# The output loop of a linear attention, reordered from two stages to three

## The chip, the cores and the metric

The kernel runs on one core of a Trainium2 chip. The core has five engines with a queue of instructions each, which they work off in order: TensorE (PE, matrix products and transposes into the PSUM memory), VectorE (DVE), ScalarE (ACT), GpSimd (POOL) and SyncE (SP, which here issues transfers). They wait for one another through semaphores. The metric is the time of one execution on the device in microseconds (us), the median of the runs.

## The reference

The input x has 4 images of 256 channels and 64 x 64 pixels, in fp32. Four layers follow, each of the form x = x + layer(groupnorm(x)):

- layer 0: a 3x3 convolution with group norm and ReLU, and on it an attention of every pixel to every pixel (4096 x 4096 logits per image, 128 channels) whose output goes through a 1x1 convolution and a group norm
- layer 1: a linear attention with 4 heads of 32 channels; this is the layer that the change touches
- layer 2: a depthwise 3x3 and a pointwise convolution with weights generated from the input
- layer 3: a pointwise convolution with a mix of 4 experts' weights

The core of layer 1:

```
xn = rmsnorm(x, g_norm)
q, k, v = split(einsum('oc,bchw->bohw', w_qkv, xn))
q = softmax(q, axis=-2); k = softmax(k, axis=-1)
context = einsum('bhdn,bhen->bhde', k, v)
out = einsum('bhde,bhdn->bhen', context, q * scale)
out = einsum('oc,bchw->bohw', w_out, out) + b_out
return rmsnorm(out, g_out)
```

The last line divides each pixel's 256 outputs by their norm. The kernel folds context and w_out into one matrix w2, so that the output of a pixel is q times w2, then takes its norm, scales by the inverse, and adds the result to x. That last part is the output loop.

## The kernel before

**Two streams of work.** The attention of layer 0 is the largest part. `attend(b)` (L596 to L659) is a generator: each step is one iteration, made of two logits matmuls (`pf`, L606), two exponentials on ACT (L607), two matmuls with the values (`py`, L645) and one running sum on DVE (`tot`). Everything else of an image, the convolution ahead of the attention and the three layers behind it (`tail`), is a second stream, written as generators that say `yield n` between their pieces. `Chain` (L39 to L78) turns each `yield n` into a credit of n times a rate, and for every whole credit one attention iteration is put between the pieces. There is no planner behind it: the order in which the program writes the instructions is the order in each engine's queue (`manual_schedule`, L1099).

**The runs.** While attention of image 0 runs, image 1 is convolved (rate 1.5). With attention of image 1 come the layers 1 to 3 of image 0 and the convolution of image 2 (rate 0.86), and with attention of image 2 the layers of image 1 and the convolution of image 3 (0.86). With attention of image 3 come the layers of image 2 (rate 1.24). The layers of image 3 come last and have no attention beside them; `alone` is true there.

**The output loop** (L791 to L836) goes over 8 chunks of 512 pixels. It has three functions:

- `outputs(c)`: four products of q with w2 go to two PSUM banks (`ps_o`, L799), ACT squares them and accumulates each pixel's sum of squares into `zr` (L801, four squares), DVE takes the maximum with 1e-24 (L803), and POOL raises it to the power -1/2 (`rsqrt`, L187; the page shows it as L189)
- `scaled(zr, banks)`: `z` is the product times `zr`, read from the two `ps_o` banks, as two operations on DVE (L814, shown as L109); with `alone` the first half is done by ACT instead (L812)
- `added(c, z)`: for each half of the channels four transposes of `z` into a bank (`ps_zt`, L822), then on DVE the sum with the residual (L823, shown as L112) and its statistics (`bn_stats`, L824)

One turn writes outputs(c), a `yield 0.6`, added(c-1), scaled(c) and another `yield 0.6`. After the last turn come a `yield 1` and added(7). After the loop the statistics of the layer are aggregated (`mv`, L276) and averaged over the group by two small matmuls on PE (`pm`, L281, and `pv`, L290), with which layer 2 begins.

**Buffers.** All banks of PSUM come from one pool of 8 (L106): `pf`, `py`, `ps_o`, `ps_zt` and the rest. The first writer of a bank waits until the last reader of its previous content is done. `zr` has three buffers, `z` comes from a pool of ten (`k4`, L95) or, alone, from alternating spare memory, and `junk` (the squares that nobody reads) has one.

Of the kernel before, what the change touches and what calls it, by code (L numbers as in the profile page):

```python
# [81 lines left out]
def conv_preact_fast(ctx: ExitStack, tc: tile.TileContext, guard, x, wc, wtpg, ww, wqkv, wout, w1cat, wd2,  # L82
# [11 lines left out]
    def k4(name):  # L94
        return wk.tile([P, CH], F32, tag="k4", name=name, bufs=10)  # L95
# [6 lines left out]
    def junk():  # L102
        return wk.tile([P, 512], F32, tag="junk", name="junk")

    def bank(name):
        return pp.tile([P, 512], F32, tag="bank", name=name, bufs=8)  # L106

    def tt(o, a, b, op):
        nc.vector.tensor_tensor(o, a, b, op)  # L109

    def stt(o, a, s, b, op0, op1):
        nc.vector.scalar_tensor_tensor(o, a, s, b, op0, op1)  # L112
# [74 lines left out]
    def rsqrt(o, v):  # L187

        nc.gpsimd.tensor_tensor(o, v, half[:, 0:v.shape[1]], ALU.pow)  # L189
# [510 lines left out]
    def linear_attention(w, b, big, qT, k4, st, sh, alone):  # L700
# [4 lines left out]
        NC = N // 512  # L705
# [54 lines left out]
        last = None  # L760
        for c in range(NC):
# [8 lines left out]
            last = this  # L770
# [22 lines left out]
        def outputs(c):  # L793
            zr = sp.tile([P, 4], F32, name="zr", bufs=3)
            banks = []
            for s in range(2):
                ps = bank("ps_o").rearrange("p (j o) -> p j o", j=2)
                for j in range(2):
                    nc.tensor.matmul(ps[:, j, :], qT[:, bass.ts(4 * c + 2 * s + j, P)], w2, start=True, stop=True)  # L799
                for j in range(2):  # L800
                    nc.scalar.activation(junk()[:, 0:NH * P], ps[:, j, :], AF.Square, accum_out=zr[:, 2 * s + j:2 * s + j + 1])  # L801
                banks.append(ps)
            nc.vector.tensor_scalar(zr, zr, 1e-24, None, ALU.max)  # L803
            rsqrt(zr, zr)
            return zr, banks

        def scaled(zr, banks):
            z = k4("z").rearrange("p (j o) -> p j o", j=4)
            for s in range(2):
                if alone and s == 0:  # L810
                    for j in range(2):
                        nc.scalar.activation(z[:, j, :], banks[0][:, j, :], AF.Copy, scale=zr[:, j:j + 1])  # L812
                    continue
                tt(z[:, bass.ts(s, 2), :], banks[s], zr[:, bass.ts(s, 2)].unsqueeze(2).to_broadcast([P, 2, NH * P]), ALU.mult)  # L814
            return z

        def added(c, z):
            cols = bass.ts(c, 512)
            for h in range(NH):
                pt = bank("ps_zt")  # L820
                for j in range(4):
                    nc.tensor.transpose(pt[:, bass.ts(j, P)], z[:, j, bass.ts(h, P)], ident)  # L822
                stt(big[:, h, cols], pt, gains[:, 1, h:h + 1], big[:, h, cols], ALU.mult, ALU.add)  # L823
                nc.vector.bn_stats(st[:, h, c, :], big[:, h, cols])  # L824

        last = None
        for c in range(NC):
            zb = outputs(c)
            yield 0.6
            if last is not None:  # L830
                added(c - 1, last)
            last = scaled(*zb)
            yield 0.6
        yield 1
        added(NC - 1, last)
        return st  # L836


# [222 lines left out]
    def tail(b, big, qT, k4=k4, diag=None, xs_in=None, held=None):  # L1061

        def layers(w):
            st, sh = yield from nonlocal_out(w, b, big, k4, xs_in)
            st = yield from linear_attention(w, b, big, qT, k4, st, sh, diag is not None)
            st, sh = yield from generated(w, b, big, k4, st, sh, diag)
            if b + 2 < B:
                load_x(b + 2)
            elif b + 2 == B:
                for h in range(NH):  # L1070
                    for q in range(2):
                        half_image = bass.ts(q, N // 2)
                        nc.sync.dma_start(out=x_cols[:, h, half_image], in_=xs_d[b + 1, h, :, half_image])
            yield from mixed(w, b, big, k4, st, sh, held)
        return layers
# [23 lines left out]
    with tc.manual_schedule(engines={E.PE, E.Activation, E.DVE, E.Pool, E.SP}):  # L1099
# [19 lines left out]
        last = end.steps()  # L1119
# [596 lines left out]
```

## Time and profile before

| | before |
|---|---|
| median of 3 runs (lowest, highest) | 3239.0 us (3237.38, 3240.34) |
| profiled execution: own time, span | 3238.86 us, 3237.0 us |
| mean clock granted to TensorE | 0.982 |
| busy: PE, DVE, ACT, POOL | 95%, 64%, 35%, 4% |
| chain that ended last: PE, DVE | 78%, 14% |
| output loop of images 0 and 1, products of chunk 0 to the aggregation | 56.2, 56.7 us |
| output loop of image 2 | 62 us |
| output loop of image 3, without attention | 39.7 us |

The span is the time from the first to the last instruction of the profiled execution; 1.9 us of its own time lie around it. A busy share is an average over stages with different limits. The stretch of the output loop of images 0 to 2 holds attention iterations of the next image as well, so its length is no measure of the loop alone.

In a line of a timeline the columns are start, duration, engine, source line, operation, output<-input, shapes, a count, and in brackets how long the engine was idle before it and which instruction ended that. A helper's line stands for all its calls: L109 is every `tt`, L112 every `stt`. Matmuls are pipelined, so the duration of a group of them overlaps the next.

### The profile page before, as it was taken

Reading aid. Unit: us, or ns where it says so; the run is one execution under the profiler, and the core shown is the slowest. Engines: PE = TensorE matmul, PEld = TensorE weight load, DVE = VectorE, ACT = ScalarE, POOL = GpSimd, SP = SyncE. Lnnn points to the kernel's source line nnn. Section 1 sums busy time; section 2 is a strip of 40 time slices with the busy share of each in tenths; the row PEclk is TensorE's granted clock in tenths of the full one; section 3 lists DMA queues with packets and bytes.
Section 4 is the critical chain, followed back from the end, with each engine's and each line's share of the span. In section 5 each row is a group of like instructions: output and inputs, shape, how many; then the busy total and the mean of one; then the engine's idle time right before and its main releaser. Section 6 shows DMA issues by size and latency. Waiting matters only on the chain.

```text
span 3237.0 us, 24205 instructions
## 1 busy us (share of the span) xinstructions
PE 3082.0 (95%) x8494; PEld 1480.6 (46%) x8494; DVE 2075.6 (64%) x2603; ACT 1146.4 (35%) x2139; POOL 129.3 (4%) x169
## 2 busy tenths in 40 slices
PE   6899989999999999999999999999999999996797
PEld 3354434445554444444465344444555534443533
DVE  8646675342546995786537796778353768855575
ACT  2232224333555332223364532222355453333520
POOL 0000000000010000000011000000000100000100
PEclk9999999999999999999999999999999999997998
DMA  5510103001100013113300102211410010121101
GB/s 178 177 36 30 33 30 59 7 13 46 66 11 20 20 72 117 36 36 65 111 10 1 39 20 82 101 44 33 107 59 1 10 33 13 46 72 46 49 0 73
DMA packets 73792, 161.66 MB, mean 50 GB/s; under 512 B 7744, under 2 KB 39232, under 8 KB 70720
## 3 DMA queue, kind: packets, MB, share of 16 engines
q1 hardware_dynamic: 69056, 143.27, 12.9%
q0 software_dynamic: 4608, 16.78, 2.9%
q8 instruction: 69, 1.13, 0.1%
q14 instruction: 59, 0.48, 0.0%
HBM read 103.40 MB, written 73.40 MB: 55 GB/s over the span
## 4 chain that ended last, share of the span: by engine, by line
PE 78%; DVE 14%; issue 5%; ACT 2%; DMA 0%; POOL 0%; SPq 0%; POOLq 0%; ACTq 0%
PE pf L606 23%; PE py L645 22%; PE ps_conv L380 8%; PE ps_qkv L734 5%; DVE dw L112 4%; PE ps_tp L582 3%; PE ps_ex L1045 3%; PE ps_pw L908 2%; DVE tot L109 2%; PE ps_g L587 2%; PE ps_h L867 2%; PE ps_wy L629 1%; PE ps_o L799 1%; DVE big L109 1%; DVE ra L112 1%
## 5 line engine op out<-in xcount | busy, mean ns | idle before, releaser
L607 ACT ACTIVATE pr<-pf 128x512 f32<-128x512 f32 x1024 | 604.0, 596 | 1241.1 <-PE pf L606 1234.0
L606 PE MATMUL pf<-tpg 128*128 128x512 f32 x2048 | 969.0, 595 | 2.8 <-ACT pr L607 2.8
L645 PE MATMUL py<-pr,tpg 128*128 128x512 f32 x2048 | 962.2, 592 | 2.9 <-ACT pr L607 2.7
L109 DVE TENSOR_TENSOR tot<-tot,pr 128x1024 f32<-128x1024 f32 x448 | 546.4, 1220 | 280.1 <-ACT pr L607 278.7
L645 PEld LDWEIGHTS py<-pr,tpg 128*128 128x128 f32 x2048 | 388.7, 190 | 494.5 <-issue 478.3
L606 PEld LDWEIGHTS pf<-tpg 128*128 128x128 f32 x2048 | 381.6, 190 | 451.4 <-issue 420.0
L380 PE MATMUL ps_conv<-v,u 128*128 128x512 f32 x576 | 267.3, 611 | 29.0 <-DVE v L109 25.1
L112 DVE SCALAR_TENSOR_TENSOR dw<-xp,dk,dw 128x1008 f32<-128x1008 f32 x224 | 282.9, 1267 | 7.0 <-ACT dw L900 3.7
L380 PEld LDWEIGHTS ps_conv<-v,u 128*128 128x128 f32 x576 | 112.0, 196 | 175.1 <-issue 141.8
L734 PE MATMUL ps_qkv<-wqkv_s,xg 128*128 128x384 f32 x384 | 130.8, 490 | 0.0
L582 PE MATMUL ps_tp<-big,wtpg_s 128*128 128x512 f32 x256 | 117.1, 601 | 3.0 <-ACT big L470 3.0
L189 POOL TENSOR_TENSOR rstd<-rstd,half 128x2 f32<-128x2 f32 x24 | 16.8, 700 | 2508.0 <-DVE rstd L292 2314.3
L109 DVE TENSOR_TENSOR tpg<-ps_g,bg_s 128x512 f32<-128x512 f32 x32 | 22.1, 691 | 146.0 <-PE ps_g L587 146.0
L908 PE MATMUL ps_pw<-dw,pk 128*128 128x512 f32 x224 | 103.8, 597 | 10.9 <-DVE dw L112 10.9
L620 DVE RECIPROCAL inv<-pss 128x512 f32<-128x512 f32 x32 | 107.2, 3351 | 8.0 <-PE pss L618 8.0
L734 PEld LDWEIGHTS ps_qkv<-wqkv_s,xg 128*128 128x128 f32 x384 | 72.2, 191 | 52.6 <-issue 8.9
L742 DVE TENSOR_REDUCE qs<-qk 128x16 f32<-128x512 f32 x24 | 16.5, 686 | 123.4 <-ACT qk L736 123.4
L109 DVE TENSOR_TENSOR v<-ra 128x1024 f32<-128x1024 f32 x72 | 86.8, 1218 | 0.4
L583 ACT ACTIVATE tpg<-ps_tp,btp_s 128x512 f32<-128x512 f32 x64 | 43.9, 687 | 119.2 <-PE ps_tp L582 119.1
L908 PEld LDWEIGHTS ps_pw<-dw,pk 128*128 128x128 f32 x224 | 42.7, 191 | 65.4 <-issue 50.9
L582 PEld LDWEIGHTS ps_tp<-big,wtpg_s 128*128 128x128 f32 x256 | 47.6, 193 | 54.5 <-issue 50.0
L801 ACT ACTIVATE junk<-ps_o 128x256 f32<-128x256 f32 x128 | 49.2, 384 | 64.5 <-PE ps_o L799 57.5
(273 smaller groups left out, 2948.3 us busy)
## 6 DMA issues: line engine op xcount, KB each, us to landing
u<-filters SPq DMA_DIRECT2D x144, 128.0 KB, 2.3
xp<-in_x_dram SPq DMA_DIRECT2D x16, 1024.0 KB, 6.4
xs_d<-big POOLq DMA_DIRECT2D x32, 512.0 KB, 11.2
wy_d<-wt SPq DMA_DIRECT2D x32, 512.0 KB, 3.0
out_dram<-res SPq DMA_DIRECT2D x64, 256.0 KB, 2.0
wy<-wy_d SPq DMA_DIRECT2D x28, 512.0 KB, 5.2
xs<-xs_d SPq DMA_DIRECT2D x24, 512.0 KB, 5.3
wp<-in_wp_dram SPq DMA_DIRECT2D x16, 512.0 KB, 4.6
```

What stands on the lines that cost most here:

```text
L109: nc.vector.tensor_tensor(o, a, b, op)
L112: nc.vector.scalar_tensor_tensor(o, a, s, b, op0, op1)
L380: nc.tensor.matmul(ps[oh], u(oh, h), v[:, bass.ts(h, 512)], start=(h == 0), stop=(h == NH - 1))
L582: nc.tensor.matmul(ps, wtpg_s[:, h, k, :], big[:, h, cols], start=(h == 0), stop=(h == NH - 1))
L587: nc.tensor.matmul(ps[:, j, :], big[:, h, bass.ts(4 * c + j, P)], wtpg_s[:, h, 2, :], start=(h == 0), stop=(h == NH - 1))
L606: nc.tensor.matmul(pf, phi[:, bass.ts(2 * m + s, P)], theta[:, bass.ts(q, 512)], start=True, stop=True)
L607: nc.scalar.activation(pr[:, bass.ts(s, 512)], pf, AF.Exp)
L620: nc.vector.reciprocal(inv, pss)
L645: nc.tensor.matmul(py, g[:, bass.ts(2 * m + s, P)], probs[i][:, bass.ts(s, 512)], start=(m == 0 and s == 0), stop=(m == NM - 1 and s == 1))
L734: nc.tensor.matmul(ps[:, 0:3 * HID], xg[:, h, bass.ts(j, P)], wqkv_s[:, h, :], start=(h == 0), stop=(h == NH - 1))
L908: nc.tensor.matmul(ps, pk[:, h * NH * P + oh * P:h * NH * P + (oh + 1) * P], dw[h][:, bass.ts(s, 512)], start=(h == 0), stop=(h == NH - 1))
L1045: nc.tensor.matmul(ps, wm[h][:, bass.ts(oh, P)], big[:, h, cols], start=(h == 0), stop=(h == NH - 1))
```

## The change

`outputs(c)` ends with the squares. The maximum and the power become a function of their own, `inverse(zr)`. The loop runs two turns longer: a turn writes the products and squares of chunk c, then the sums of chunk c-2, then the inverse of chunk c and the scaling of chunk c-1. In the two added turns only the parts that are left are written, with one `yield 0.6` each; the `yield 1` ahead of the last sums is gone. The credits of the loop go from 8 x 1.2 + 1 = 10.6 to 8 x 1.2 + 2 x 0.6 = 10.8. The two `ps_o` banks of a chunk are read by its scaling one turn later. The instructions themselves are the same.

```diff
                     nc.scalar.activation(junk()[:, 0:NH * P], ps[:, j, :], AF.Square, accum_out=zr[:, 2 * s + j:2 * s + j + 1])
                 banks.append(ps)
+            return zr, banks
+
+        def inverse(zr):
             nc.vector.tensor_scalar(zr, zr, 1e-24, None, ALU.max)
             rsqrt(zr, zr)
-            return zr, banks
...
-        last = None
-        for c in range(NC):
-            zb = outputs(c)
+        zb, z = {}, {}
+        for c in range(NC + 2):
+            if c < NC:
+                zb[c] = outputs(c)
+                yield 0.6
+            if c > 1:
+                added(c - 2, z.pop(c - 2))
+            if c < NC:
+                inverse(zb[c][0])
+            if 0 < c <= NC:
+                z[c - 1] = scaled(*zb.pop(c - 1))
             yield 0.6
-            if last is not None:
-                added(c - 1, last)
-            last = scaled(*zb)
-            yield 0.6
-        yield 1
-        added(NC - 1, last)
         return st
```

## The prediction

> **What bounds the kernel now.** I read the shares of busy time first, then windows laid on the four executions of the output loop, then the timelines of TensorE (PE) and VectorE (DVE) in them, and last the stretches that follow. The shares, from the page's first part (busy us, share of the span, instructions):
>
> ```profile
> PE 3082.0 (95%) x8494; PEld 1480.6 (46%) x8494; DVE 2075.6 (64%) x2603; ACT 1146.4 (35%) x2139; POOL 129.3 (4%) x169
> ```
>
> TensorE sets the end; its gaps are worth something, nobody else's are as such. Busy times in the windows of the loop (start:end and length; then PE, its weight loads, DVE, ACT, POOL with instructions; clock, DMA share, GB/s), of batches 0, 2 and 3 (batch 1 is like batch 0):
>
> ```profile
> 946.77:1003.00 56.23, 55.47 (x208) 33.80 (x208) 42.83 (x66) 26.66 (x84) 11.61 (x8) 1.00 0.00 1
> ...
> 2528.00:2590.00 62.00, 62.00 (x207) 33.39 (x206) 45.25 (x74) 24.52 (x67) 9.93 (x6) 1.00 0.00 1
> 3030.32:3070.06 39.74, 27.39 (x128) 20.49 (x128) 28.50 (x50) 21.25 (x80) 8.06 (x8) 0.89 0.26 85
> ```
>
> In three of four executions attention of the next batch runs between the chunks and PE is busy 98 to 100%: no wait is there to remove. Only batch 3 runs alone, with PE busy 27.4 of 39.7 us. At the end of the loop of batch 0 (DVE's timeline, then PE's):
>
> ```profile
> 997.15 0.69 DVE L824 BATCH_NORM_STATS2 st<-big 128x6 f32<-128x512 f32 x1
> 997.76 1.27 DVE L109 TENSOR_TENSOR z<-ps_o,zr 128x512 f32<-128x512 f32 x2
> 998.94 1.21 DVE L109 TENSOR_TENSOR tot<-tot,pr 128x1024 f32<-128x1024 f32 x1
> ```
>
> ```profile
> 998.48 0.44 PE L822 MATMUL ps_zt<-ident,z 128*128 128x128 f32 x2 [0.60 <-DVE z L109]
> 999.08 0.88 PE L822 MATMUL ps_zt<-ident,z 128*128 128x128 f32 x6 [0.16 <-DVE z L109]
> 999.79 1.88 PE L606 MATMUL pf<-tpg 128*128 128x512 f32 x4
> ```
>
> The last z stands behind the four operations of added(6) on DVE; an attention iteration on PE hides all of that but 0.76 us. Batch 3, timeline of one turn:
>
> ```profile
> 3059.10 1.01 POOL L189 TENSOR_TENSOR zr<-zr,half 128x4 f32<-128x4 f32 x1 [3.10 <-DVE zr L803]
> ...
> 3060.14 0.84 ACT L812 ACTIVATE rt<-ps_o,zr 128x256 f32<-128x256 f32 x2 [1.39 <-POOL zr L189]
> ...
> 3061.63 0.67 DVE L109 TENSOR_TENSOR rt<-ps_o,zr 128x512 f32<-128x512 f32 x1
> ...
> 3062.36 0.87 PE L822 MATMUL ps_zt<-ident,rt 128*128 128x128 f32 x6 [1.00 <-DVE rt L109]
> ```
>
> Here ScalarE (ACT) does wait 1.39 us a turn for the inverse root. A turn is 4.11 us: four squares 2.03, max, hand-over and pow 1.24, two scalings 0.84.
>
> PE in the convolution after it (timeline; the pm/pv pair is the normalization's mean and variance):
>
> ```profile
> 1402.97 3.27 PE L380 MATMUL ps_conv<-v,u 128*128 128x512 f32 x7 [2.17 <-DVE v L109]
> ...
> 1466.11 6.35 PE L380 MATMUL ps_conv<-v,u 128*128 128x512 f32 x9 [4.41 <-DVE v L109]
> ...
> 1493.59 0.38 PE L290 MATMUL pv<-ev,avg 128*128 128x2 f32 x2 [0.84 <-DVE ev L109]
> ```
>
> After an idle 2.17 us, 7 matmuls take 3.27; after 4.41 us, 9 take 6.35 where 9 x 0.43 + 0.16 = 4.0 would do: 2.3 us more are lost to a slower clock.
>
> [...] gaps of 2.17 and 2.57 us left matmuls at 0.43 us, gaps of 2.76 and up (3.02, 3.86, 4.41) brought some at 0.85. [...] no trace view shows banks, the code takes all 8 from one pool (L106). [...] the pow takes 1.01 us in batch 3, 1.45 on average in batch 0.
>
> **The change part by part.** No operation is added or taken away; the order within each engine's queue changes.
>
> *The inverse comes a chunk before its use.* In batches 0 to 2 it gains nothing: in the 955 to 995 stretch of batch 0 the groups of lines show 12 z and 56 transposes with 0.0 us idle ahead of them; the attention of the next batch covers the pow (with that cover gone it costs what batch 3 shows, 1.39 us a turn). In batch 3 ACT's 1.39 us wait goes. What is late next: DVE does added(c-1), then max, then z(c), and PE's transposes need z(c) before the next added(c). One turn is then 2 x (0.77 + 0.62) = 2.77 for added, 0.08 for max beside it, 0.65 for half of z, and z to transposes to first sum 0.46 to 0.73: 3.96 to 4.23 us against 4.11. So the DVE loop takes the pow's place; the steady gain is nothing. With the first turns (squares run ahead) and the last one I get the first sum of chunk 7 at 3065.1 instead of 3067.2: -2.1 us (-0.6 to -2.5).
>
> *The last turns lose an attention iteration.* Credits: before 8 x 1.2 + 1 = 10.6 with a whole 1 between the last scaled and the last added; now 10.8 with 0.6 there. At rate 0.86 this is 0.52 of an iteration, and in batches 0 and 1 none falls between the transposes of chunks 6 and 7 in PE's order of instructions (before: one). Walk from the start E of the products of chunk 7 (attention on PE 3.44 us, products 1.73, eight transposes 0.87: start to start in the timeline, as 1.72 from pf at 999.79 to py): transposes of 5 end at E+2.60, attention at 6.04, transposes of 6, held 0.26 by z(6), at 7.2. DVE: tot ends 7.5, added(6) 2.78 to 10.3, first half of z(7) 0.67 to 10.96. PE waits from 7.2 to 11.0, 3.8 us, and 0.4 for z's second half. Queued behind the waiting transposes stand the logits of two attention iterations, and ACT's exponentials wait for those. The displaced iteration is not lost, it runs behind them, but it hides nothing there. Minus the 0.76 of before: +3.4. A gap of 3.8 us is past the point of the half clock: +2.1. The mean's pm and pv now stand side by side too (an attention parted them): 0.84 as in the 1493.59 line, +0.8. First turns, where a logits matmul waits for a bank that the products still hold one chunk longer: 0.7 against 0.5, +0.2. Sum +6.5 each, +13.0 for two.
>
> *Batch 2, rate 1.24.* Here transposes of 5 and 6 are side by side; those of 6 wait for z(6) behind added(5): 3.2 us, half clock 2.2. Twice (after the transposes of 1 and of 3) products come directly ahead of a logits matmul whose bank is freed only by the second sum: 0.75 each. Sum +6.9; before, nothing.
>
> *Banks in the steady turns.* Four banks of products are held instead of two. In batches 0 and 1 the second logits matmul gets the bank of the transposes just written, freed by its first sum: some 0.4 us before PE wants it. I cost it at nothing; the cover is that 0.4 us.
>
> *What shifts behind the loop.* 0.2 more credits and one step less of delay put what follows up to one attention earlier or later against the layer. In the taps, where DVE is busy 104.7 of 106 us and PE waits little for it: +0.4 each for two batches. In the convolutions of batches 2 and 3: the 2.17 gap gets an attention ahead of it and goes, the 0.84 at pv too, the 4.41 turns to about 3.3 with about 1 elsewhere: -3.0; taken as -2.5 each, since one more attention can open another gap (-5 to +3). DMA issues keep their places relative to the layer; the loop itself issues none.
>
> *Sum.* 13.0 + 6.9 - 2.1 + 0.8 - 5.0 = +13.6 on the profiled execution's 3238.9 (span 3237.0 and 1.9 around it), which is 0.1 below the median of 3239.0: 3252.5.
>
> **Rivals.**
> - *The clock stays full.* The waits come, the slow matmuls don't (gaps shorter than the 2.57 to 2.76 us between which the trace changes over). For: the walk to batch 2's gap is 3.2, close. Against: every gap from 2.76 up brought slow ones. 13.6 - 2 x 2.1 - 2.2 = +7.2: 3246.
> - *The convolution gives it back* (not slower). The loop's loss is as said, but the shifted attention fills both stalls of each convolution: 2.17 + 4.41 + 2.3 of clock + 0.84 = 9.7 each, 19.4 in all, against 18.6 lost: -0.8, 3238. It decides from where one iteration more stands directly ahead of the 4.41 stall: 3.44 us of cover leave 1.0, below the half clock. Against: the twelve DVE operations that cause it move as well.
> - *A bank wait in each turn.* The 0.4 us of slack is not there, and some 0.5 us is lost in 7 turns of 3 batches: +10, 3262. For: it is thin, and estimated from durations. Against: DVE has 43 of 56 us to do.
> - *The change does what it says* in batch 3, and the DVE loop does not bind: a turn at 3.5 us, -4.3 instead of -2.1: 3250, no other verdict.
>
> **How the numbers follow.** Forecast 0.50 (with the last rival in it; alone 3246 to 3258), clock full 0.15, convolution gives back 0.20, bank waits 0.15. A measurement of this kernel can tell about 0.2%, 6.5 us, from no change. Slower: all but little of the forecast and of the bank case, half of the clock case: 0.70. Same: most of the convolution case, half of the clock case: 0.20. Faster: the far side of the convolution case, and waits that I see and that don't come: 0.10. The range, 3239 to 3263, takes in half of the convolution case and most of the bank case.
>
> **What would show it.** Right: in batches 0 and 1 a PE idle of some 3.8 us ahead of the last transposes, put down to DVE's z, and matmuls near 0.85 us after it; in batch 2 one of 3.2 us ahead of the transposes of chunk 6; in batch 3 no ACT wait for POOL's root, but about 4 us a turn, PE waiting for z. The 2.17 gap of the convolution gone. Wrong: those idle times under 2 us (then the walk of DVE is wrong), a convolution free of its 4.41 us stall, or logits waiting for banks in every turn.

## The result

| | before | after |
|---|---|---|
| median of the runs (lowest to highest) | 3238.62 us (3237.38 to 3240.34) | 3256.94 us (3256.69 to 3258.07) |
| span of the profiled execution | 3237.0 us | 3255.3 us |
| PE busy | 3082.0 us | 3088.1 us |
| DVE, ACT busy | 2075.6, 1146.4 us | 2077.4, 1147.7 us |

The changed kernel is slower: ratio 1.0057, 95% interval 1.0039 to 1.0074, or 18.3 us of the medians. No engine but PE has more to do, and PE's own busy time grew by only 6 us: the rest is idle time on PE.

Windows on the output loops of images 0, 2 and 3 after the change, each from the products of chunk 0 to the first matmul of the mean (start:end, length, then PE, its weight loads, DVE, ACT, POOL with instructions, granted clock, DMA share, GB/s), and last the same window of image 2 before the change:

```profile
947.06:1013.53 66.47, 62.27 (x218) 36.67 (x219) 45.23 (x71) 27.92 (x86) 8.06 (x8) 0.97 0.00 1
...
2518.10:2600.20 82.10, 78.09 (x256) 43.20 (x255) 54.91 (x77) 33.95 (x98) 8.06 (x8) 0.98 0.03 10
3050.95:3089.75 38.80, 24.87 (x128) 19.46 (x129) 29.07 (x52) 21.48 (x80) 8.06 (x8) 0.90 0.29 94
...
2504.44:2579.33 74.89, 74.89 (x255) 42.59 (x254) 53.58 (x77) 33.79 (x98) 14.07 (x8) 1.00 0.03 11
```

The last line puts one reading right. The window 2528:2590, from which the 62 us for image 2 were taken, misses the start of its loop (6 of the 8 pows lie in it) and goes on past its end; the whole loop took 74.9 us before, with PE busy all the time, and takes 82.1 now. That PE had nothing to lose there stays true.

The lines of the changed kernel have other numbers: the maximum is L806, ACT's scaling L814, the transposes L824, the statistics L826.

In images 0 and 2 PE is idle for 4 us, where before, in the same windows, it was idle for 1 us and not at all. The end of the loop of image 0, timeline of PE, and under it that of DVE:

```profile
1002.98 0.44 PE L824 MATMUL ps_zt<-ident,z 128*128 128x128 f32 x2 [3.62 <-DVE z L109]
1003.58 1.54 PE L824 MATMUL ps_zt<-ident,z 128*128 128x128 f32 x6 [0.16 <-DVE z L109]
1004.92 2.77 PE L606 MATMUL pf<-tpg 128*128 128x512 f32 x4
```

```profile
1001.65 0.69 DVE L826 BATCH_NORM_STATS2 st<-big 128x6 f32<-128x512 f32 x1
1002.26 1.27 DVE L109 TENSOR_TENSOR z<-ps_o,zr 128x512 f32<-128x512 f32 x2
```

The last transposes stand idle for 3.62 us until z(7) comes, and z(7) stands on DVE behind the last operation of the sums of chunk 6 (that one begins at 1001.65 and takes 0.69 us; z begins at 1002.26, with no idle on DVE). The four records of the two logits matmuls after it take 2.77 us at a granted clock of 0.68 (1004.92:1007.69), where before they took 1.88 at 1.00 (the 999.79 line of before). Image 2 has the same thing one chunk earlier (PE):

```profile
2586.09 1.63 PE L824 MATMUL ps_zt<-ident,z 128*128 128x128 f32 x8 [3.27 <-DVE z L109]
```

For every stage I summed from PE's records what is lost: idle (between two records more than 0.03 us) and slow (the time from start to start beyond the usual of the same line and shape, idle left out). An idle also leaves about 0.16 us in the slow share, because a record with nothing behind it lasts 0.59 us where the usual step is 0.43. "Taps" is from the mean to the last pointwise matmul of layer 2; "mixed" goes to the first convolution matmul; "projection" from the last of these to the last `ps_g`; "next layer 1" from there to the next output loop. In us, for images 0 and 1:

| stage | before | after | difference |
|---|---|---|---|
| output loop | 1.8, 1.8 | 7.0, 7.2 | +5.3, +5.5 |
| taps | 2.5, 2.5 | 5.8, 5.8 | +3.3, +3.3 |
| mixed | 4.1, 4.1 | 4.5, 4.5 | +0.4, +0.4 |
| convolution | 11.4, 11.4 | 6.5, 6.6 | -4.9, -4.8 |
| projection | 2.8, 2.8 | 6.2, 6.1 | +3.4, +3.3 |
| next layer 1 | 6.6, 1.0 | 4.9, 1.0 | -1.7, 0.0 |

The loop of image 2 adds 7.2, that of image 3 takes 38.80 us instead of 40.58 (-1.8), the rest of image 3 takes 1.3 less, small items 0.1 more. The sum is 5.8 + 7.7 + 7.2 - 1.8 - 1.3 + 0.1 = 17.7; PE's last matmul lies 17.6 us later.

### The profile page after: what moved, and what is told of

The parts are those of the page before. It is cut to its first block, busy times and chain, and to the rows that moved or that the text cites. A ratio compares the mean times of both kernels' runs of the same rounds, so it can differ in the third digit from the quotient of the medians.

```text
span 3255.3 us, 24169 instructions
## 1 busy us (share of the span) xinstructions
PE 3088.1 (95%) x8494; PEld 1482.3 (46%) x8494; DVE 2077.4 (64%) x2603; ACT 1147.7 (35%) x2139; POOL 116.2 (4%) x169
## 4 chain that ended last, share of the span: by engine, by line
PE 76%; DVE 16%; issue 5%; ACT 2%; DMA 0%; POOL 0%; SPq 0%; POOLq 0%; ACTq 0%
PE pf L606 22%; PE py L645 22%; PE ps_conv L380 7%; PE ps_qkv L734 5%; DVE dw L112 4%; PE ps_tp L582 3%; PE ps_ex L1050 3%; PE ps_pw L913 2%; DVE tot L109 2%; PE ps_h L872 2%; PE ps_g L587 2%; PE ps_wy L629 2%; PE ps_o L799 1%; DVE big L112 1%; DVE ra L112 1%
## 5 line engine op out<-in xcount | busy, mean ns | idle before, releaser
L380 PE MATMUL ps_conv<-v,u 128*128 128x512 f32 x576 | 270.3, 615 | 22.1 <-DVE v L109 18.3
L736 ACT ACTIVATE qk<-ps_qkv,rinv 128x256 f32<-128x256 f32 x96 | 45.4, 473 | 73.7 <-PE ps_qkv L734 70.5
```

Of the source, the lines that this page charges most:

```text
L380: nc.tensor.matmul(ps[oh], u(oh, h), v[:, bass.ts(h, 512)], start=(h == 0), stop=(h == NH - 1))
```

## The experiments

Each was timed against the kernel before on the same chip, whose median there was 3238 to 3239.4 us.

**Credits of before in the changed kernel.** It keeps the transposes side by side, but everything behind the loop stands as in before.

```diff
             if 0 < c <= NC:
                 z[c - 1] = scaled(*zb.pop(c - 1))
-            yield 0.6
+            if c <= NC:
+                yield 1 if c == NC else 0.6
```

> The changed kernel with the credits of before (1 between the last scaling and the last sums, 10.6 in all). In PE's order the transposes of chunks 6 and 7 (images 0, 1) and of 5 and 6 (image 2) still stand side by side, while all that follows the loop stands against the attention as in before. Theory (the waits in the loop and the shift behind it are two separate losses): the idle of 3.6 us ahead of the last transposes stays, the taps, convolutions and projections lose what they lose in before; 3238.6 + 2 x 5.1 (loops of images 0 and 1) + 6.8 (image 2) - 2.2 (image 3) = 3253.4. Rival (the wait in the loop makes what is lost behind it, too): as after, 3256.9.

Measured 3253.9 us, ratio 1.0047 (1.0030 to 1.0064). PE's timeline, loop of image 0:

```profile
1001.34 2.14 PE L824 MATMUL ps_zt<-ident,z 128*128 128x128 f32 x8 [3.61 <-DVE z L109]
```

The wait is there, the loops lose 7.0 and 7.2 us; taps 2.4, mixed 4.1, projection 2.9 and 2.8 are those of before. The convolutions lose 12.5 and 13.1, 1.2 and 1.7 more than before, at the same idle times. So the wait in the loop is one loss and what lies behind it another. It is the stages that show this and not the time: the four executions lie at 3251.3, 3252.0, 3255.8 and 3256.1 us, which reaches from the theory's 3253.4 to the rival's 3256.9, and the profile is of the third.

**The kernel before with 0.2 more credit.** The other half: no side-by-side transposes, but the shift.

```diff
-        yield 1
+        yield 1.2
         added(NC - 1, last)
```

> The kernel before with 0.2 more credit ahead of the last sums (10.8 as after): two stages, no side-by-side transposes, but the shift behind the loop as in after. Theory (two separate losses): PE idle in the loops as in before or 0.8 us less each; behind them the idle of after: 0.84 at pv, 0.9 at the softmax sum, 1.6 at the attention's output product, about 2.1 and 2.8 in each convolution; 3238.6 + 3.4 - 2 x 0.8 = 3240.4. Rival (the shift alone costs nothing): 3238.6 or, with the idle of the loops gone, 3237.0.

Measured 3233.4 us, ratio 0.9987 (0.9980 to 0.9994): it is faster, not slower. PE in the taps of image 0:

```profile
1080.69 1.13 PE L618 MATMUL pss<-inv,ones 128*128 128x512 f32 x2 [0.94 <-DVE inv L614]
...
1161.56 1.98 PE L629 MATMUL ps_wy<-yt,ww_s 128*128 128x512 f32 x4 [1.63 <-DVE yt L109]
```

The idle behind the loop is as I expected and nearly as in after: taps lose 5.9, convolutions 6.5 and 6.2, projections 6.2 and 4.8, the next layer 1 4.9. This settles that the shift makes them, not the wait. Taken together, against before, they are +0.6 for each of the two images. The expected time missed elsewhere. The two loops lose 0.1 us instead of 1.8 (two attention iterations now stand ahead of the last transposes), which I had at -0.8 each; and image 3 takes 3.3 us less. I took its instructions to be in the same order as before. In its output loop and its last layer they are, but not in layer 2, whose depthwise and pointwise products alternate otherwise with the other credit. PE in layer 2 of image 3, two lines of before, then two of this version:

```profile
3094.87 25.76 PE L943 MATMUL ps_dw<-xp,tpg 128*128 128x512 f32 x56 [2.76 <-ACT tpg L955]
3124.05 1.12 PE L908 MATMUL ps_pw<-dw,pk 128*128 128x512 f32 x2 [2.57 <-DVE dw L112]
...
3090.82 27.46 PE L943 MATMUL ps_dw<-xp,tpg 128*128 128x512 f32 x60 [2.76 <-ACT tpg L955]
3120.01 1.12 PE L908 MATMUL ps_pw<-dw,pk 128*128 128x512 f32 x2 [0.87 <-DVE dw L112]
```

From the loop's end to the last pointwise product PE's idle falls from 17.4 to 15.4 us with this order, and 1.2 us more of slow matmuls take part of it back. The other 2.5 us, in the loop and the last layer, come with less of slow matmuls.

**The kernel before once more**, to see whether those 3.3 us are chance. The expectation was written in the belief that the order is the same.

> The kernel before once more, unchanged. In its first profile the layers of image 3 behind the loop took 159.5 us; in the profile of the version with 0.2 more credit, whose instructions for image 3 stand in the same order, they took 157.0, and the loop 39.8 instead of 40.6. Theory ([...] the same order takes another time from run to run): this profile differs from the first by about 1 us or more in image 3, with the same idle times. Rival (the order before image 3 decides it): 40.6 and 159.5 again.

Measured 3238.85 us, ratio 1.0 (0.999 to 1.001). The difference that my theory expected did not come: from the first output loop on, every stage of this profile is as long as in the first to some hundredths of a us (loop of image 3 40.55, behind it 159.51). That doesn't show the rival, for executions of one program do differ: of the 19 with 0.2 more credit, 12 took 3231.5 to 3234.5 us and 7 took 3236.8 to 3237.5, and the profile is of the first group. And up to the first output loop PE's order is the same in all the versions here and its idle is 38.9 us in each profile, but by the same count its slow matmuls (without the ends at the idles) cost 9.7 to 11.3 us, and the loop begins at 945.2 to 947.1. So how much of the 3.3 us belongs to the credit stays open. In the last layer of image 3, where the order is the same, both have 3.22 us idle, and the slow share is 4.91 us in before and 3.24 with the credit; what decides that wasn't tried.

**Throwaway transposes during the wait** (images 0 and 1; image 2 left as it is).

```diff
                 pt = bank("ps_zt")
+                if c == NC - 1 and h == 0 and w.rate < 1:
+                    for _ in range(32):
+                        nc.tensor.transpose(pt[:, 0:P], ident, ident)
```

> The changed kernel with 32 transposes of the identity, whose result is written over, ahead of the transposes of chunk 7 in images 0 and 1; PE does them while z(7) is late. Image 2 is left as it is, as a control. Theory (the wait costs its length and then a slow clock): the idle ahead of the last transposes falls from 3.6 us to about 0.1, their end doesn't move, the matmuls behind them run at 0.43 us and the slow share of the loops of images 0 and 1 goes from 2.8 and 3.0 us to about 0.5; 3256.9 - 2 x 2.4 = 3252. Rival (the slow matmuls come from something else in this place): slow shares and time unchanged, 3257.

Measured 3250.6 us, ratio 1.0034 (1.0022 to 1.0047), 6.4 us less than after (7.1 when each is taken against the kernel before on its own chip). PE in the loop of image 0, then the start of the convolution behind it:

```profile
997.64 3.66 PE L825 MATMUL ps_zt<-ident 128*128 128x128 f32 x32
1001.43 0.44 PE L827 MATMUL ps_zt<-ident,z 128*128 128x128 f32 x2
...
1002.74 1.88 PE L606 MATMUL pf<-tpg 128*128 128x512 f32 x4
...
1310.53 3.70 PE L380 MATMUL ps_conv<-v,u 128*128 128x512 f32 x8 [2.12 <-DVE v L109]
```

The logits are back at 1.88 us (2.77 in after), so the slow matmuls in the loop came from the idle. They cost 1.5 and 1.7 us per loop (slow share 2.8 and 3.0 to 1.3), not the 2.4 that I expected; image 2, the control, keeps its 3.2. The other part of the gain is in the convolutions, 1.9 and 1.7 us: the idle of 2.12 us is followed by 8 matmuls in 3.70 us, and in after by 8 in 5.40 us. That this part is the throwaway transposes' doing isn't shown. They stand some 300 us ahead of it, and the version with 0.2 more credit, which has none, has both in one execution, PE at the start of the convolution behind the loop of image 0, and then of image 1:

```profile
1305.95 5.40 PE L380 MATMUL ps_conv<-v,u 128*128 128x512 f32 x8 [2.12 <-DVE v L109]
...
2069.38 3.70 PE L380 MATMUL ps_conv<-v,u 128*128 128x512 f32 x8 [2.12 <-DVE v L109]
```

**Three stages for image 3 alone**, two for the others: the loop of before stands under the new condition.

```diff
+        if not alone:
...
+            added(NC - 1, last)
+            return st
         zb, z = {}, {}
         for c in range(NC + 2):
```

> Three stages for image 3 alone (no attention beside it), two for the others as before. Theory (DVE's loop z, transposes, sums takes the place of the pow): turns of 4.05 us instead of 4.11, ACT no longer waits for POOL, PE waits 1.2 us a turn for DVE's z; 3238.6 - 2.2 = 3236.4. Rival (the pow was the limit and its time is gained in full, 1.39 us a turn): 3238.6 - 8 x 1.39 = 3227.5.

Measured 3235.7 us, ratio 0.9992 (0.9983 to 1.0001), not clear of nothing in the time; its loop of image 3 takes 38.80 us as in after (40.58 before). One turn of that loop, timeline of after, which has the same turn:

```profile
3068.39 0.15 DVE L806 TENSOR_SCALAR zr<-zr 128x4 f32<-128x4 f32 x1
3068.45 0.68 DVE L109 TENSOR_TENSOR z<-ps_o,zr 128x512 f32<-128x512 f32 x1
...
3069.19 0.87 PE L824 MATMUL ps_zt<-ident,z 128*128 128x128 f32 x6 [1.23 <-DVE z L109]
3069.66 0.75 DVE L112 SCALAR_TENSOR_TENSOR tpg<-ps_zt,gains,tpg 128x512 f32<-128x512 f32 x1 [0.53 <-PE ps_zt L824]
```

A turn is 3069.66 - 3065.61 = 4.05 us (the sum before this one begins at 3065.61). It is the DVE loop of the prediction: sums, z, PE's transposes, sums. The pow is no longer part of what sets the turn, but the loop that takes its place is as long, so the steady turn gains next to nothing (4.05 us against 4.11).

**Scaling ahead of the sums, image 3 alone.**

```diff
-            if c > 1:
-                added(c - 2, z.pop(c - 2))
-            if c < NC:
-                inverse(zb[c][0])
             if 0 < c <= NC:
                 z[c - 1] = scaled(*zb.pop(c - 1))
+            if c > 1:
+                added(c - 2, z.pop(c - 2))
+            if c < NC:
+                inverse(zb[c][0])
```

> Three stages for image 3 alone, and in each of its turns the scaling of chunk c-1 ahead of the sums of chunk c-2, so that a transpose never waits for a z behind the sums of the chunk before; two stages for the others as before. Theory (that place of z closes DVE's loop): turns of 2.77 + 0.65 + 0.08 = 3.5 us, DVE without idle; about -0.6 x 8 more than the version without the swap: 3238.6 - 2.2 - 4.4 = 3232.0. Rival (another engine holds the turn at 4.05): 3236.4.

Measured 3236.4 us, ratio 0.9994 (0.9985 to 1.0002): neither theory named what came, and that the time equals the rival's 3236.4 is luck. The loop takes 41.76 us, 1.2 more than before, and what lies behind it 155.9, 3.6 less. Timeline of one turn:

```profile
3054.14 0.15 DVE L806 TENSOR_SCALAR zr<-zr 128x4 f32<-128x4 f32 x1
3054.44 1.01 POOL L189 TENSOR_TENSOR zr<-zr,half 128x4 f32<-128x4 f32 x1 [3.70 <-DVE zr L806]
3055.48 0.69 DVE L109 TENSOR_TENSOR z<-ps_o,zr 128x512 f32<-128x512 f32 x1 [1.18 <-POOL zr L189]
```

The maximum is now DVE's last operation of a turn and z its first of the next, so the pow stands between them with nothing to cover it: a turn is 4.71 us (3050.77 to 3055.48), and DVE is idle for 1.18.

**Scaling, inverse, sums, image 3 alone.** The three stages as in the last version, the inverse moved ahead of the sums:

```diff
             if 0 < c <= NC:
                 z[c - 1] = scaled(*zb.pop(c - 1))
+            if c < NC:
+                inverse(zb[c][0])
             if c > 1:
                 added(c - 2, z.pop(c - 2))
-            if c < NC:
-                inverse(zb[c][0])
```

> As the version with the scaling ahead of the sums for image 3 alone, with the inverse between the two: scaling of c-1, inverse of c, sums of c-2; two stages for the other images. Theory (a turn of image 3 is bound by DVE's own work once neither the pow nor z, transposes, sums closes its loop): max 0.15 + z 0.65 + sums 2.77 = 3.6 us a turn, DVE without idle, the loop of image 3 from 40.6 us of before to about 36.5; 3238.4 - 4 = 3234. Rival (squares and scaling of ACT, or banks, hold the turn at 4.05 or more): as three stages alone in the order of after, 3235.7.

Measured 3228.9 us, ratio 0.9971 (0.9960 to 0.9983). Timeline of DVE over one turn:

```profile
3046.12 0.67 DVE L109 TENSOR_TENSOR rt<-ps_o,zr 128x512 f32<-128x512 f32 x1
3046.71 0.16 DVE L806 TENSOR_SCALAR zr<-zr 128x4 f32<-128x4 f32 x1
3046.78 0.75 DVE L112 SCALAR_TENSOR_TENSOR tpg<-ps_zt,gains,tpg 128x512 f32<-128x512 f32 x1
...
3049.55 0.67 DVE L109 TENSOR_TENSOR z<-ps_o,zr 128x512 f32<-128x512 f32 x1
```

No line of the turn carries a wait; it is 3.43 us of DVE's own work, and the sums (2.77 us) cover the pow. The loop of image 3 takes 34.86 us, 5.7 less than before (the first theory had 4), and what lies behind it 156.0 instead of 159.5, which neither theory had: 1.9 us less idle, 1.6 less slow matmuls. The short turn isn't what makes that part, for the version before this one, with the longest turn, had 155.9, and the next one, with this same turn, 158.2. The three stages carry 0.2 more credit, and layer 2 of image 3 has the other order of products here too. This version beats both kernels.

**The same order in all images.** PE's order is exactly that of after.

> The changed kernel with the order scaling of c-1, inverse of c, sums of c-2 in all images. PE's order is that of after, the transposes of chunks 6 and 7 (5 and 6 in image 2) side by side. Theory (they wait only because z stands behind the sums of the chunk before on DVE): no idle over 0.5 us ahead of them, loops of images 0 to 2 lose under 1 us each instead of 7; behind the loop as after; 3256.9 - 2 x 6.2 - 7 - 2.5 (image 3) = 3235. Rival (side by side, they wait for banks, or for transposes of another chunk, whatever z does): 3250 or more.

Measured 3232.1 us, ratio 0.9980 (0.9971 to 0.9988), 24.8 us below after. End of the loop of image 0, PE and then DVE (`tot` is a running sum of the attention):

```profile
997.74 1.38 PE L824 MATMUL ps_zt<-ident,z 128*128 128x128 f32 x8 [0.95 <-DVE z L109]
```

```profile
995.79 1.21 DVE L109 TENSOR_TENSOR tot<-tot,pr 128x1024 f32<-128x1024 f32 x1
996.91 1.28 DVE L109 TENSOR_TENSOR z<-ps_o,zr 128x512 f32<-128x512 f32 x2
998.11 0.74 DVE L112 SCALAR_TENSOR_TENSOR big<-ps_zt,gains,big 128x512 f32<-128x512 f32 x1
```

The side-by-side transposes wait 0.95 us instead of 3.62, more than the 0.5 that I had, since z(7) still stands behind that running sum. The loops lose 1.6, 1.6 and 0.4 us instead of 7.0, 7.2 and 7.2. With PE's order unchanged, the order on DVE alone, z and the inverse ahead of the sums, takes the loss out of the loops. Three stages in all images are still 3.3 us longer than in image 3 alone (3228.9): beside attention they gain nothing, for the loops of images 0 to 2 lost 1.8, 1.8 and 0 us in before.

**Two stages with 0.2 more credit, and the good three stages for image 3.** The edits of two versions above together.

> Two stages for images 0 to 2 with 0.2 more credit ahead of the last sums (10.8), three stages for image 3 in the order scaling, inverse, sums. Theory (the gains add): loops of images 0 and 1 without idle (-1.7 each), behind them +0.6 and +0.6 as with the credit alone, image 3 -4; 3238.4 - 2.2 - 4 = 3232. Rival (the credit's 4.9 us were gained in image 3 by the clock, and aren't a gain of the credit): 3234 to 3236.

Measured 3228.7 us, ratio 0.9969 (0.9957 to 0.9980), no better than without the credit (3228.9). The loops of images 0 and 1 lose 0.1 us and the loop of image 3 takes 34.85, but layer 2 and 3 of image 3 take 158.2 us where the version without the credit takes 156.0. In these two profiles the gains don't add: behind the loop of image 3 PE has the same order and 0.7 us less idle with the credit, but 2.9 us more of slow matmuls. 3232 was too high all the same, as the three stages bring 5.7 us, not 4.

## Why the prediction was right or wrong

It had 3252, range 3239 to 3263, slower at 0.70; measured 3256.9. The waits in the loops came by the mechanism that it named; behind the loops of images 0 and 1 it had a gain of 4.2 us, and a loss of 1.1 came; there one step of it failed.

**The last turns lose an attention iteration: right.** The walk gave 3.8 us of idle ahead of the transposes of chunk 7; measured were 3.62, and 0.16 (not 0.4) for z's second half. The term of the slow clock was 2.1; the slow share of the two loops grew by 2.1 and 2.3 (2.8 and 3.0 against 0.7), of which the throwaway transposes take away 1.5 and 1.7. Loop and the pm/pv pair together: predicted +6.5 per image, measured 5.3 and 5.5 in the loop and 0.84 at pv, so 6.1 and 6.3.

**Image 2: right.** Predicted +6.9, measured +7.2; the idle 3.27 instead of 3.2. The two bank waits were mis-sized, 0.32 (0.06 and 0.26) instead of 0.75 each. What made up for it is a term that it left out: the slow share was 3.2, of which 2.2 are slow matmuls, as predicted, and 1.0 the ends of the records ahead of six idles. So the sum came out by luck in part.

**The inverse a chunk earlier: right, but for one sign.** Image 3 gained 1.8 us in the loop (predicted 2.1); the DVE loop took the pow's place at 4.05 us a turn (predicted 3.96 to 4.23). The sign "no ACT wait for POOL's root" was wrong: ACT still waits 0.77 us for it in each turn, since the maximum is late on DVE, but ACT isn't in the loop that sets the turn.

**Banks in the steady turns: right.** No turn of images 0 and 1 but the first ones shows a logits matmul that waits for a bank; that rival is out.

**What shifts behind the loop: the step that failed.** For the taps I took +0.4; it was +2.5 without pv. That the shift makes this, and not the wait in the loop, is what the two half versions above show. The products that end a block of attention met a DVE busy with the taps:

```profile
1088.29 1.13 PE L618 MATMUL pss<-inv,ones 128*128 128x512 f32 x2 [0.94 <-DVE inv L614]
...
1169.14 1.98 PE L629 MATMUL ps_wy<-yt,ww_s 128*128 128x512 f32 x4 [1.62 <-DVE yt L109]
```

I had looked at where layer 2's own matmuls would wait, and not at the softmax sum and the output product of the attention, which wait for operations in the same DVE queue. For the convolutions I took -2.5 each, as the stalls themselves; the stretch from the first convolution matmul gave back 4.9 and 4.8, and the projection behind it took 3.4 and 3.3 again:

```profile
1313.53 5.40 PE L380 MATMUL ps_conv<-v,u 128*128 128x512 f32 x8 [2.12 <-DVE v L109]
...
1474.52 5.28 PE L380 MATMUL ps_conv<-v,u 128*128 128x512 f32 x8 [2.81 <-DVE v L109]
```

The idle times of 2.17 and 0.84 did go, and the 4.41 fell to 2.81 (I had 3.3); but the group mean ahead of the projection waits 1.66 us and two value products 1.6 and 1.8 for ACT (before: 0.8 at pv and 1.2 once), which I hadn't worked through. Taps, mixed, convolution, projection and next layer 1 without pv come to -0.3 for image 0 and +1.4 for image 1, where I had -2.1 each. That is 5.3 us. From profile to profile the change costs 18.2 us where I had 13.6, so the forecast was 4.6 too low, and the other terms cancel but for 0.7; among them are 1.3 us that image 3 saved behind its loop, at which I had nothing.

**The rivals.** "The clock stays full" is out: behind the three long waits in the loops (3.62, 3.62 and 3.27 us) the next four records of logits take 2.77, 3.50 and 3.36 us at a granted clock of 0.68, 0.52 and 0.56. "The convolution gives it back" happened in part: the 4.41 us stall was shortened, and paid for in the projection. "The change does what it says" in image 3, with a turn of 3.5 us, is out for this order (4.05), and true for the order scaling, inverse, sums (3.43).

## What to carry to other kernels

When a stage is put between two others, look at what stands ahead of the critical operation in each engine's queue, not only at the distance between the stages: here the same three stages cost 18 us or gain 6 to 7 depending on whether the scaling and the inverse stand behind the sums or ahead of them, and gain 10 where only image 3, which has no attention beside it, gets them. In the first and last turns of a software pipeline, count which filler work is left between two steps that depend on each other; that is where the wait came. A shift of the two streams by one iteration changes waits far behind the change, so walk the closing steps of both streams, and test the shift by itself, which one changed credit does.

## What the runs showed of the hardware

- **Idle time alone doesn't tell whether slow matmuls follow.** Behind the 2.17 us in before's convolution 8 matmuls took 3.70 us at a granted clock of 1.00 (1402.97:1406.67); behind the 2.12 us in after's 8 took 5.40 at 0.68 (1313.53:1318.93); and in one execution of the version with 0.2 more credit, behind the same 2.12 us, 8 took 5.40 in the convolution behind the loop of image 0 and 3.70 in the one behind that of image 1. The limit that the prediction read from before alone, between 2.57 and 2.76 us, doesn't hold.
- **In the traces of before and after the granted clock is 1.00 or 0.50, and its changes, 25 and 31 of them, lie whole multiples of 3.413 us apart.** Behind the 3.62 us of image 0's loop in after it is 0.50 from 1003.29 to 1006.70, behind the 2.12 us from 1313.90 to 1317.32. Those 2.12 us (1311.41 to 1313.53) lie inside one step of the grid (1310.49 to 1313.90); before's 2.17 us (1400.80 to 1402.97) are parted by the grid point at 1402.35. Whether that decides if slow matmuls follow isn't shown; no run tests it.
- **Two executions can differ in slow matmuls where the order and the idle are the same.** Up to the first output loop all profiles have the same order on PE and 38.9 us idle, but 9.7 to 11.3 us of slow matmuls. The two profiles of the kernel before agree within some hundredths of a us in every stage behind that point, so a second profile that agrees isn't proof.
- **The pow on POOL takes 1.01 us in every turn of after (8.06 us for 8), where before it averaged 1.45 in images 0 and 1.** In each of those two loops of before the four pows that lie beside a running sum `tot` on DVE for about 1 us took 1.85 to 1.91 us (the one at 950.27, `tot` at 950.10), and the four beside the sums of a chunk 1.01. In after none lies beside a running sum for more than 0.14 us. Whether the running sum lengthens the pow wasn't tried by itself.
